# Layer 0's state-space mixer: the scan of a chunk's decays is pinned to its written place in VectorE's order

## The chip, the core and the metric

The kernel runs on one core of a Trainium2 chip. The metric is device microseconds (us) for one execution of the whole program, four layers deep; the time of a kernel is the median of its runs. Lower is better.

## The reference, cut to what matters

Four layers act on x, 4 sequences of 512 tokens with 256 channels. Each layer computes `x = x + attn(xn) + ffn(xn)` with `xn = layernorm(x)`. The change lies in layer 0, whose "attention" is a state-space mixer (Mamba2) with 32 heads of 64 channels and a state of 128. For each head and token t the reference does

```
h = dA[t] * h + (dt[t] * x[t]) (outer) B[t]
y[t] = h . C[t]
```

and then adds `D * x`, multiplies by silu(gate), normalises and projects back to 256 channels. Beside it, layer 0 has a gated feed-forward (256 to 1024 to 256) on the same xn. Layers 1 to 3 (latent attention with product-key experts; a head mixer with routed experts; full attention with top-p experts) are not touched.

## The kernel before, in words

**Tiling.** The recurrence over time is cut into chunks of 128 tokens. Work goes by group of 8 heads: 4 sequences x 4 groups = 16 groups `i`, each with 4 chunks `t`, so 64 chunks `c = 4i + t`. Inside a chunk the recurrence becomes matrix products: `G[s, h, t]`, the product of the decays from token s to token t, times `CB`, the product of B and C, is a 128x128 matrix for each head, and `y = G' x` (L486). What earlier chunks contribute comes through the state `S` (L468, L476, L481, L482).

**How G is made.** `decays` (L403) loads the chunk's decay rows from DRAM, broadcast to 128 partitions (tile `G`, 3 buffers, 512 KB a load, issued on SyncE's queue, SP, L406). `before` (L413) runs a scan on VectorE (DVE) over it with an identity as second operand (L421): it turns the row of single decays into running products, 128x1024 elements, in place. `before_gpsimd` (L443) multiplies by `CB` on GpSimd (POOL, L447). TensorE (PE) reads the result in L486, which frees the buffer.

**The loop.** `mamba_pieces` is software-pipelined by hand. The body for chunk c issues, in written order: for the next group, two projections (t = 0) or one (t = 1, 2) or none (t = 3) (`group`, L134, with ScalarE, ACT, at L276 and L400); the load of G for chunk c+2 (`decays`); the scan for chunk c+1 and its transposes (`before`, L421, L427, L429 and the loads of `eb`, L437); the convolution taps of the projections on DVE (L280, three for each projection); `within` for chunk c (L468, L469, L470 on POOL, G times CB for chunk c+1 on POOL L447, `xw` for chunk c+1 on POOL L450, L476, S, L486, then L491 and L492 on DVE, and the `ssq` sums on POOL, L496 to L499); and `project_out` for chunk c-1 (L507, added on DVE at L513). The feed-forward (L134 with tile `wu`, L201, L202, L212, added to x on DVE at L158) is woven in between by `weave`, which gives the next piece to the stream that is furthest behind by hand-written costs. After four groups of one sequence, the result is normalised (L152) and, when the feed-forward is also through, layernormed (L102, L103, L110).

**What sets the order on an engine.** Each engine runs its instructions strictly in a listed order and waits at the first one that isn't ready. The framework's scheduler makes these lists: it may move an instruction against its neighbours of the same engine as data dependencies and buffers allow. `tc.keep_in_program_order(...)` pins an instruction to its written place among the pinned ones. In the kernel before, the eight matmuls of L486 and the add L491 of each chunk are pinned; the scan L421 is not.

**PSUM.** The pools are "mm" with 4 buffers, "tr" with 2 and "acc" with 2. "tr" is shared by the transposes L427 (freed by L429), the projection L507 (freed by L513) and the feed-forward's output L212 (freed by L158).

Of the kernel before, what the change touches and what calls it, by code (L numbers as in the profile page):

```python
# [82 lines left out]
def v3(ap, b):  # L83
    return ap.rearrange("p (a b) -> p a b", b=b)
# [161 lines left out]
def mamba_pieces(c, a, ws, open_pool):  # L246
# [4 lines left out]
    nc, tc = c.nc, c.tc  # L251
# [161 lines left out]
    def before(i, t):  # L413

        b, g = i // 4, i % 4
        CT, Btok, CB, acc, ssq = seqs[b]
        w, wo, xc, sg = groups[i]
        tt, hs, cols = b * TPB + t, slice(g * HG, (g + 1) * HG), slice(t * P, (t + 1) * P)
        G = Gs.pop((i, t))
        flat = G.rearrange("p h t -> p (h t)")  # L420
        nc.vector.tensor_tensor_scan(  # L421
            flat, flat, eye.rearrange("p h t -> p (h t)"), 0.0, ALU.mult, ALU.add
        )

        pt = c.ps("tr")
        for k in range(4):
            nc.tensor.transpose(pt[:, k * P : (k + 1) * P], xc[:, k, cols], c.ident)  # L427
        xdt = c.tile(pool, [P, 512], "xdt")
        nc.vector.tensor_mul(v3(xdt, HD), v3(pt, HD), by_head(dt[:, tt, hs]))  # L429
        eb = None  # L430
        xD = c.tile(pool, [P, 4, P], "xD")
        for k in range(4):
            nc.scalar.mul(xD[:, k, :], xc[:, k, cols], d_par[:, 4 * g + k : 4 * g + k + 1])  # L433
        if t > 0:
            eb = c.tile(pool, [P, 4, P], "eb")
            for half in range(2):
                nc.sync.dma_start(  # L437
                    eb[half * HD : (half + 1) * HD],
                    since[tt, g * HG + half : (g + 1) * HG : 2, :].partition_broadcast(HD),
                )  # L440
        chunks[i, t] = [G, xdt, None, xD, eb]
# [93 lines left out]
    decays(0, 0)  # L535
    decays(0, 1)
    before(0, 0)
    before_gpsimd(0, 0)
    behind = None
    for i in range(16):  # L540
        for t in range(TPB):
            if t == 1 and i % 4 == 3 and i < 15:
                yield from sequence(i // 4 + 1)
            taps = []
            for k in ((0, 1), (2,), (3,), ())[t] if i < 15 else ():
                taps.append(group(i + 1, k))
                yield 3.4
            n = 4 * i + t + 1
            if n < 63:
                decays((n + 1) // 4, (n + 1) % 4)  # L550
            if n < 64:
                before(n // 4, n % 4)
            yield 0.5
            for tap in taps:
                tap()
            y = within(i, t)
            yield 2.6
            if behind:
                project_out(*behind)
                yield 1.7  # L560
            behind = i, t, y
# [1246 lines left out]
```

## Time and profile before

| what | us |
| --- | --- |
| median of 3 runs | 3154.67 (3148.51 to 3159.28) |
| the profiled execution's own time | 3156.7 |
| its span in the trace | 3154.9 |
| layer 0's scans, first to last start | 77.2 to 801.9 |
| PE busy in 100 to 800 | 683.5 of 700 |
| DVE busy in 100 to 800 | 549.4 of 700 |
| mean granted TensorE clock | 0.992 |

A row of the trace gives start, duration, engine, source line, output tile and inputs, and, where the engine stood idle before, for how long and on what. Matmul rows overlap, since they are pipelined: their starts count more than their durations. A PE row of 128x512 starts 0.43 us after the one before it when nothing holds PE up, though the row says 0.6 us. The four lines L427, L468, L476, L486 tell which chunk PE is at: t = 0 has no L468, t = 3 has no L476.

### The profile page before, as it was taken

The page shows a single profiled execution, that of the slowest core. Times are in us where ns is not written, and L with a number is a line of the kernel's source. Part 1 is how long each engine was busy: PE and PEld are TensorE (multiplying, and loading weights), DVE is VectorE, ACT ScalarE, POOL GpSimd, SP SyncE. Part 2 cuts the span into 40 slices and gives each one's busy share as a digit, 9 for nine tenths or more (in the row PEclk, how much of TensorE's full clock was granted, in tenths as well). Part 3 has the DMA queues.
Part 4 walks back from the last instruction along what each step waited for, and adds up shares of the span by engine and source line. Part 5 has one row for each costly group of instructions (what it writes and reads, how often), then busy time and mean ns, then how long its engine had stood idle before and what let it go on. Part 6 is the DMA issues. An engine that isn't in the chain of part 4 may idle for free.

```text
span 3154.9 us, 35717 instructions
## 1 busy us (share of the span) xinstructions
PE 3082.5 (98%) x12502; PEld 1885.9 (60%) x12502; DVE 1841.9 (58%) x4656; ACT 1249.8 (40%) x2898; POOL 627.9 (20%) x521
## 2 busy tenths in 40 slices
PE   8999999999899999999999999999999999999999
PEld 5566566565655555555676656566566655555555
DVE  5778778777677787787666555554555522222222
ACT  4444435444356666666525333333333311111111
POOL 0465455555400123331223000000000000000000
PEclk9999999999899999999999999999999999999999
DMA  4233333332310234444233000000000000000000
GB/s 131 77 100 124 93 94 111 103 104 77 118 37 13 80 99 117 101 112 138 80 100 103 4 21 7 1 27 1 21 1 1 20 21 20 20 20 20 0 0 27
DMA packets 89090, 185.15 MB, mean 59 GB/s; under 512 B 14192, under 2 KB 57216, under 8 KB 84176
## 3 DMA queue, kind: packets, MB, share of 16 engines
q1 hardware_dynamic: 74448, 135.05, 13.4%
q0 software_dynamic: 14176, 47.01, 6.2%
q8 instruction: 99, 1.62, 0.2%
q10 hardware_dynamic: 288, 0.82, 0.1%
q14 instruction: 79, 0.65, 0.1%
HBM read 160.95 MB, written 12.98 MB: 55 GB/s over the span
## 4 chain that ended last, share of the span: by engine, by line
PE 79%; DVE 11%; DMA 5%; ACT 2%; POOL 2%; issue 2%; SPq 1%; DVEq 0%; ACTq 0%; POOLq 0%
PE mm L134 30%; PE acc L212 9%; PE mm L643 7%; PE mm L142 5%; PE acc L1116 4%; PE acc L659 4%; DMA G<-own 3%; DVE G L421 2%; PE tr L1108 2%; DVE cy L280 2%; PE tr L824 2%; PE tr L507 2%; PE acc L868 2%; PE mm L1446 1%; PE tr L212 1%
## 5 line engine op out<-in xcount | busy, mean ns | idle before, releaser
L134 PE MATMUL mm<-xnT,wu 128*128 128x512 f32 x2128 | 953.3, 595 | 4.2 <-DVE cy L280 2.0
L134 PEld LDWEIGHTS mm<-xnT,wu 128*128 128x128 f32 x2128 | 399.3, 191 | 468.7 <-issue 435.8
L650 ACT ACTIVATE pr<-pr,nm 128x128 f32<-128x128 f32 (+3 forms) x512 | 285.7, 558 | 306.9 <-DVE nm L646 304.5
L202 DVE TENSOR_TENSOR hT<-sg,mm 128x512 f32<-128x512 f32 x176 | 120.6, 685 | 386.3 <-PE mm L134 372.1
L201 ACT ACTIVATE sg<-mm 128x512 f32<-128x512 f32 x176 | 104.6, 594 | 591.5 <-PE mm L134 591.3
L646 DVE CUSTOM_DVE_ANT_0 pr<-mm,late 128x128 f32<-128x128 f32 (+3 forms) x512 | 245.4, 483 | 82.6 <-PE mm L643 80.9
L212 PE MATMUL acc<-wu,hT 128*128 128x256 f32 x1280 | 286.6, 380 | 0.3 <-DVE hT L167 0.3
L212 PEld LDWEIGHTS acc<-wu,hT 128*128 128x128 f32 x1280 | 241.7, 190 | 49.1 <-issue 17.7
L134 PE MATMUL mm<-xnT,w_in 128*128 128x512 f32 x512 | 230.8, 597 | 0.0
L986 POOL DMA_INDIRECT e<-in_p_experts,ids x128 | 128.4, 1003 | 454.1 <-DVE x L152 413.4
L421 DVE TENSOR_TENSOR_SCAN G<-G,eye 128x1024 f32<-128x1024 f32 x64 | 156.0, 2437 | 64.9 <-DMA G<-own 64.8
L447 POOL TENSOR_TENSOR G<-G,CB 128x1024 f32<-128x1024 f32 x64 | 151.5, 2368 | 172.3 <-DVE G L421 95.9
L643 PE MATMUL mm<-kf,qf 128*128 128x128 f32 (+3 forms) x512 | 177.2, 445 | 6.1 <-DVE qf L801 3.7
L280 DVE SCALAR_TENSOR_TENSOR cy<-mm,ws,cy 128x511 f32<-128x511 f32 (+2 forms) x216 | 158.6, 741 | 34.9 <-ACT cy L276 31.4
L643 PE MATMUL mm<-k,q 128*128 128x128 f32 (+3 forms) x512 | 176.5, 434 | 1.0 <-DVE q L1081 1.0
L134 PEld LDWEIGHTS mm<-xnT,w_in 128*128 128x128 f32 x512 | 97.5, 192 | 103.3 <-issue 97.2
L433 ACT ACTIVATE xD<-xc,ws 128x128 f32<-128x128 f32 x256 | 84.2, 391 | 180.6 <-POOL y L470 164.2
L152 DVE SCALAR_TENSOR_TENSOR x<-acc,cw,x 128x256 f32<-128x256 f32 x128 | 62.0, 484 | 153.6 <-PE acc L212 153.5
L1116 PE MATMUL acc<-PT,V 128*128 128x512 f32 (+3 forms) x512 | 149.1, 433 | 0.0
L1081 DVE TENSOR_SCALAR q<-mm,bias 128x512 f32<-128x512 f32 x64 | 48.0, 751 | 165.1 <-PE mm L134 165.1
L824 PEld LDWEIGHTS tr<-con,pr 128*128 128x128 f32 x640 | 79.4, 142 | 95.0 <-ACT pr L817 30.2
L507 PE MATMUL tr<-wo,y 128*128 128x256 f32 x512 | 126.5, 390 | 6.9 <-DVE x L158 3.8
(310 smaller groups left out, 4926.8 us busy)
## 6 DMA issues: line engine op xcount, KB each, us to landing
G<-own SPq DMA_DIRECT2D x64, 512.0 KB, 4.4
w_in<-in_m_units SPq DMA_DIRECT2D x16, 1024.0 KB, 5.1
eb<-since SPq DMA_DIRECT2D x96, 128.0 KB, 3.4
wu<-in_o_units SPq DMA_DIRECT2D x8, 1536.0 KB, 6.5
wo<-in_m_units SPq DMA_DIRECT2D x16, 512.0 KB, 4.1
psw<-pes SPq DMA_DIRECT2D x128, 64.0 KB, 2.8
wu<-in_g_units SPq DMA_DIRECT2D x4, 1536.0 KB, 6.8
wu<-in_f_units SPq DMA_DIRECT2D x4, 1536.0 KB, 7.3
```

Of the source, the lines that this page charges most:

```text
L134: c.nc.tensor.matmul(out, lhsT=w[:, d, cols], rhs=c.xnT[:, d, tokens], start=(d == 0), stop=(d == 1))
L142: c.nc.tensor.matmul(out, lhsT=c.xnT[:, d, tokens], rhs=w[:, d, cols], start=(d == 0), stop=(d == 1))
L212: nc.tensor.matmul(po[:, j, :], lhsT=hT[k][:, (t + j) * P : (t + j + 1) * P], rhs=wd[:, k, :], start=(i == 0), stop=(i == per - 1),)
L280: nc.vector.scalar_tensor_tensor(y[:, j:], src[:, : SEQ - j], conv[:, k, 3 - j : 4 - j], y[:, j:], ALU.mult, ALU.add,)
L421: nc.vector.tensor_tensor_scan(flat, flat, eye.rearrange("p h t -> p (h t)"), 0.0, ALU.mult, ALU.add)
L447: nc.gpsimd.tensor_mul(G, G, seqs[b][2][:, t, :][:, None, :].to_broadcast([P, HG, P]))
L507: nc.tensor.matmul(po, lhsT=y[:, k, :], rhs=groups[i][1][:, k, :], start=(k == 0), stop=(k == 3))
L643: nc.tensor.matmul(sc, lhsT=q[:, i * P : n], rhs=k[:, :n], start=True, stop=True)
L646: nc.vector.tensor_tensor_reduce(out=pr, in0=sc, in1=late[:, SEQ - n :], scale=1.0, scalar=-NEG, op0=ALU.add, op1=ALU.min, accum_out=nm,)
L650: nc.scalar.activation(pr, pr, AF.Exp, bias=nm, scale=-1.0, accum_out=total)
L824: nc.tensor.transpose(pt[:, (i - j) * P : (i - j + 1) * P], prs[s][i][:, j * P : (j + 1) * P], c.ident)
L1116: nc.tensor.matmul(z[:, j * P :], lhsT=head["V"][:, j, h, :], rhs=head["PT"][:, j, j * P :], start=(j == 0), stop=(j == TPB - 1),)
```

## The change

One call is wrapped: the scan of `before` is pinned.

```diff
-        nc.vector.tensor_tensor_scan(
+        tc.keep_in_program_order(nc.vector.tensor_tensor_scan(
             flat, flat, eye.rearrange("p h t -> p (h t)"), 0.0, ALU.mult, ALU.add
-        )
+        ))
```

No instruction is added or taken away on DVE: both lists have the same 64 scans and the same shapes. What moves, by the two kernels' instruction lists:

- DVE before: nearly everywhere the slot after L492 of chunk c-1 holds the scan of chunk c+2, one chunk ahead of its written place, in front of the taps and of L429 of body c. In t = 3 bodies the slot is after L469 instead.
- DVE after: that slot holds the scan of chunk c+1. In t = 3 bodies it stands ahead of L429 and L469. At the start of layer 0, three scans stood among the taps of the first group; after, the taps come first, then one scan, L158, L429, then the second scan.
- Near the end of layer 0, two adds L158 (and L513 after them) stood behind a scan; after, they stand ahead of it. The last scan stands two chunks before the end in the list before, and one chunk later in the list after.
- Where a layernorm falls into layer 0, the scan that stood ahead of it in the list before stands behind it in one place in the list after.
- POOL follows: each G times CB (L447) is that of chunk c+1 and not of chunk c+2. In t = 3 bodies the list before has `xw` (L450), `y` (L470), then G; the list after has G, `xw`, `y`.
- SP keeps the order of the G loads; some halves of the `eb` loads (L437) move across a G load. PE, ACT: single neighbours swap, on PE mostly at the hand-over to layer 1.

## The prediction

> **What bounds the kernel now.** I read the page's busy shares first, then what PE waited for inside layer 0, then what DVE waited for there, then the timeline at the gaps.
>
> ```profile
> PE 3082.5 (98%) x12502; PEld 1885.9 (60%) x12502; DVE 1841.9 (58%) x4656; ACT 1249.8 (40%) x2898; POOL 627.9 (20%) x521
> ```
>
> PE is busy for 3082.5 of 3154.9 us, and in layer 0 its matmuls start back to back. So a change can give only what PE loses: its waits, and the slower clock after them. The view of PE's waits between 100 and 780 us:
>
> ```profile
> PE tr L507 <- DVE x L158: 3.8, 2, 2.3
> PE tr L507 <- DVE acc L513: 2.7, 3, 1.0
> PE tr L368 <- ACT BT L284: 2.6, 2, 1.9
> PE mm L134 <- DVE cy L280: 2.0, 3, 1.2
> PE tr L121 <- DVE xdt L429: 1.0, 1, 1.0
> PE mm L134 <- ACT sg L400: 0.6, 1, 0.6
> ```
>
> (Total us, times, longest.) They add up to 12.7 us. At the start (77 to 100 us) PE waits 2.4 us more, for ACT xc L284, and between 780 and 815 us 7.2 us, twice for L158. All of it in layer 0's loop: 22.3 us, 0.7% of the span. Nearly all lead to a late DVE, and DVE's waits in the same 100 to 780 us say what makes it late:
>
> ```profile
> DVE G L421 <- DMA G<-own: 62.3, 42, 2.9
> DVE y L491 <- POOL y L470: 36.8, 37, 3.6
> ```
>
> 42 scans stand at the head of DVE's list before their data has landed. The mechanism, at the largest gap of the middle, in the timeline (start, duration, engine, line, and idle before it):
>
> ```profile
> 694.44 2.29 DVE L421 TENSOR_TENSOR_SCAN G<-G,eye 128x1024 f32<-128x1024 f32 x1 [2.90 <-DMA G<-own]
> 696.65 0.67 DVE L158 TENSOR_TENSOR x<-tr,x 128x512 f32<-128x512 f32 x1
> 697.37 2.92 PE L507 MATMUL tr<-wo,y 128*128 128x256 f32 x8 [2.28 <-DVE x L158]
> ```
>
> The scan, of chunk c+2, waits 2.90 us for its load, issued only when L486 of chunk c-1 had freed the buffer. L158 is ready but queued behind it, it holds a "tr" buffer, and PE stands for 2.28 us.
>
> **The change, part by part.** DVE gains and loses no instruction; each slot gets the scan of one chunk less ahead. The load of that chunk was issued one body earlier (64 chunks lie in 95 to 815 us, 11.3 us each) and lands 4.4 us after its issue by the page's DMA table: about 7 us to spare. I cost the scans' waits as gone.
>
> *1. The first group (70 to 100 us).* Three scans (2.28 at 77.22, 2.28 at 83.34, 4.03 at 86.18) stand among the taps that PE's first transposes need. After, the last three taps are bound by their ACT L276, which ends at 87.24: taps to 89.5, xc L284 by 90.2, and the last transpose can follow PE's L212, which ends at 91.7, instead of starting at 94.57. PE's waits of 0.54 and 1.90 there go. The granted clock is 0.83 in 90 to 100, and the next 16 matmuls took 8.38 us where 16 elsewhere take 7.03: 1.35 more. Gain 0.54 + 1.90 + 1.35 = **3.8**. Late next: the first L486 needs scan (to 91.8) and POOL (2.36, to 94.2), while PE has 16 projections (6.9 us) in front of it: covered.
>
> *2. The middle (100 to 780 us).* Six PE gaps stand directly behind a scan that waited (gap | the scan's wait): at 362.6 1.49 | 1.83, at 435.3 0.66 | 1.48, at 595.7 0.82 | 0.90, at 621.1 1.92 | 2.90, at 697.4 2.28 | 2.90, at 742.8 0.82 | 1.26. The scan's wait is the longer one in each, so all six go: **8.0**. The one at 697.4 also lowers the clock (0.91 and 0.92 in 690 to 710): 2.92 us against 1.99 for the same 8 matmuls, then 7.63 against 7.03: **1.5**. The other 4.7 of the 12.7 come in bodies with six taps or beside a layernorm (232, 372 to 380, 419), where DVE has work and not a wait just before; earlier waits made it late, but not alone. I take half, **2.3**; ends 0 and 4.7.
>
> *3. The bodies with t = 3.* Here a new wait comes. POOL now has scan, then G, then xw, then y in front of L491; before, y was added first:
>
> ```profile
> 131.31 0.68 DVE L469 TENSOR_TENSOR y<-acc,eb 128x512 f32<-128x512 f32 x1
> ...
> 133.21 1.26 POOL L470 TENSOR_TENSOR y<-y,xD 128x512 f32<-128x512 f32 x1
> 133.50 3.13 DVE L421 TENSOR_TENSOR_SCAN G<-G,eye 128x1024 f32<-128x1024 f32 x1 [1.51 <-DMA G<-own]
> ...
> 136.55 0.66 DVE L491 TENSOR_TENSOR y<-acc,y 128x512 f32<-128x512 f32 x1
> 136.77 2.35 POOL L447 TENSOR_TENSOR G<-G,CB 128x1024 f32<-128x1024 f32 x1 [2.30 <-DVE G L421]
> 137.25 2.43 DVE L492 TENSOR_TENSOR y<-y,sg 128x512 f32<-128x512 f32 x1
> ```
>
> Before, from the end of the t = 2 body at 130.79 to the end of L492 at 139.68: 8.9 us, with a wait of 1.51, a scan stretched to 3.13 and L492 stretched from 0.69 to 2.43 beside POOL's G. After: 2.29 + 0.1 + 2.36 + 1.04 + 1.26 + 0.03 + 0.69 + 0.69 = 8.5, since POOL is idle at L492. Three other t = 3 bodies (from 173.4, 269.0 and 458.1) took 9.1 each. So DVE stands about 3.4 us waiting for POOL, but is not later than before: **0**, ends -2 and the rival below.
>
> *4. The last four chunks (780 to 820 us).* The two gaps behind L158 (3.51 and 3.70) shrink, because L158 now stands ahead of its scan. But DVE is the bound here (no projections for PE to do), it runs four scans where it ran three, and POOL's G and xw are next to be late. Followed by hand with the rows' durations from 783.3 us, where L492 ends: scan at 784.3, PE waits for xw till 790, L158 at 797.4, scans at 798.5 and 807.3, S by 804 and 812.7, and the last L469 at 815.6, where it was at 817.54. Gain **2**; ends -3 and 7.2 + 3.2 (the clock's 0.85 and 0.83 there: 1.12 + 1.49 + 1.35 against 0.60 + 0.68 + 1.09, and as much again) = 10.
>
> *5. SP, ACT and PE lists.* Neighbours swap; the eb loads have over a body of lead. Layer 1 simply starts earlier. 0, ends -2 and 2.
>
> Sum: 3.8 + 8.0 + 1.5 + 2.3 + 0 + 2 = 17.6. The profiled execution took 3156.7 (span 3154.9 and 1.8 around it), so 3139.1; it stands 2.0 above the median of the three runs, so on the median's scale **3137**.
>
> **Two rules of the Trainium skill.** "TensorE: Matmul & The Clock Gate", section on HAM oscillation, says that PE drops to half clock only when it idles for more than about 3.4 us. The clock row of 690 to 710 us shows a drop after 2.28 us, so here the trace decides; by the rule alone the clock terms of the gaps at 94 and 697 would be no gain of this change, and the sum 2.9 less. "SBUF — State Buffer", section on who interferes with whom, speaks against the change: a VectorE operation with two SBUF inputs and a GpSimd operation that reads SBUF exclude each other for a whole instruction. The 3.13 us scan beside POOL's y above fits it. After, the scan in t = 3 bodies starts while POOL has two ssq adds of 0.73 to run; by the rule each could hold the scan up by as much, which would turn the -0.4 of part 3 into about +0.3.
>
> **Rivals.**
>
> *PE never waits.* All 22.3 us go, with the clock's 1.35 + 1.5 + 3.2: 28.4, so 3126. For it: DVE is busy only 549 of 700 us and loses 62.3 waiting for loads. Against: the tail has one scan more, and the layernorm's burst is still DVE work.
>
> *The wait only changes its name.* DVE's gain in t = 0 to 2 is eaten by the wait for POOL in t = 3, and PE's gaps move rather than go; only the start gains: 3154.7 - 3.8 = 3151. For it: the rows from 303 to 313 us, where DVE, 1.36 us earlier, would wait for ACT L276 at 306.4 and gain nothing. Against: the six gaps each end with the scan's wait.
>
> *Slower.* In the t = 3 bodies L492 stays stretched (2.43 for 0.69) although POOL's G comes earlier, because ssq or xw meet it. Then DVE is 8.5 + 1.7 - 9.0 = 1.2 us later at 15 hand-overs to a t = 0 body. The point from which it decides: at 327 us the first taps end at 326.90 and PE takes their "mm" buffer at 327.29, 0.4 us to spare, so 0.8 us of it reaches PE: 12 us, and with the tail's end at -3 and the start's 3.8: 11 slower, 3166. Against: POOL is idle 1 to 3 us before each ssq in that place.
>
> That the pin does nothing is excluded: the instruction lists differ in nearly all 64 slots.
>
> **Chances.** Forecast 0.55 (own range 3129 to 3146), PE never waits 0.15, name changes 0.18, slower 0.12. From 3123 to 3157 all but the slower one and some edges are held. 0.3%, 9.5 us, is about what a measurement of this kernel can tell from no change: below 3145.2 lie 0.50 of the forecast and the first rival, 0.65; within, 0.05 + 0.18 and a little of the slower case, 0.25; above 3164.1, 0.10.
>
> **What would show it.** Right: DVE's wait for DMA at L421 falls from 64.8 us to under 10; the six gaps are missing; PE's waits in 100 to 780 fall from 12.7 to 2 to 4; the last L469 of layer 0 comes some 17 us earlier. POOL's y grows as DVE's releaser to 60 or more: part 3. Wrong: PE waiting for L280 in every t = 0 body (slower), or G times CB as the releaser of L486.

## The result, and the profile after

The change made the kernel slightly slower. Fifteen runs of the changed kernel have a median of 3164.6 us (3156.29 to 3171.02), fifteen of the kernel before beside them 3157.49 us (3148.51 to 3166.84): a ratio of 1.0022, 95% interval 1.0011 to 1.0032. The forecast was 3137 us with a range up to 3157, so both the time and the range missed. The profiled execution took 3165.98 us (span 3164.2), 9.3 more than that of before.

From the page, the busy shares, the group of POOL's products and that of the scans (busy us, mean ns of one, and the idle time before them):

```profile
PE 3085.8 (98%) x12502; PEld 1888.4 (60%) x12502; DVE 1837.0 (58%) x4656; ACT 1245.6 (39%) x2898; POOL 637.8 (20%) x521
...
L447 POOL TENSOR_TENSOR G<-G,CB 128x1024 f32<-128x1024 f32 x64 | 151.9, 2374 | 245.9 <-DVE G L421 245.9
...
L421 DVE TENSOR_TENSOR_SCAN G<-G,eye 128x1024 f32<-128x1024 f32 x64 | 155.7, 2432 | 0.0
```

The same two groups before:

```profile
L421 DVE TENSOR_TENSOR_SCAN G<-G,eye 128x1024 f32<-128x1024 f32 x64 | 156.0, 2437 | 64.9 <-DMA G<-own 64.8
L447 POOL TENSOR_TENSOR G<-G,CB 128x1024 f32<-128x1024 f32 x64 | 151.5, 2368 | 172.3 <-DVE G L421 95.9
```

The scan's line now ends in 0.0: VectorE's 64.8 us of waits for the loads are gone entirely. In the POOL line, 245.9 us of idle time are ended by the scan, where it was 95.9: POOL's product G times CB runs as soon as its scan has ended. VectorE's waits in layer 0 (95 to 830 us; total us, times, longest):

```profile
DVE y L491 <- POOL y L470: 81.8, 44, 4.7
DVE cy L280 <- ACT cy L276: 39.8, 30, 1.6
```

The wait for POOL's y has nearly doubled, from 42.2 us. And PE's waits between 60 and 860 us, the longest ones:

```profile
PE acc L468 <- DVE S L482: 6.7, 4, 2.9
PE mm L134 <- DMA tok<-xn_tokens: 4.0, 1, 4.0
PE tr L368 <- ACT BT L284: 4.0, 3, 1.6
PE mm L476 <- POOL xw L450: 3.4, 2, 3.1
PE tr L121 <- DVE xdt L429: 3.1, 1, 3.1
```

Of the two groups at L507 that led the list of before only 0.3 us is left. New names stand in their place: S (L482), xw (L450) and xdt (L429). Between 100 and 780 us PE's gaps add up to 16.2 us, where before had 12.7.

**Where the time went.** PE's order is nearly the same in both kernels, so the start of the eight L486 of a chunk can be laid side by side, chunk by chunk (0 to 63), and then layer 1's first projection, L134 of `pw`. The comparison is aligned at the first PE gap (L134 for ACT sg, at 71.85 us before and 71.94 after). A negative number is earlier than before:

| at | after minus before, us | what happened since the row above |
| --- | --- | --- |
| chunk 0 | -4.3 | the start's gain |
| chunk 3 | -2.7 | gap at L468 for S, 1.32 |
| chunk 23 | +0.6 | gaps of 1.19 and 1.25, others |
| chunk 24 | -4.2 | gaps of before at 362 to 380 us missing |
| chunk 33 | -1.2 | gaps of 1.35, 1.16 and 1.25 |
| chunk 34 | +3.8 | L121 for xdt, 3.14, and a slower clock behind it |
| chunk 58 | -0.2 | gaps of before at 595, 697 and 743 us missing or smaller, new ones elsewhere |
| layer 1's first L134 | +7.1 | the tail |

So the start gained what was forecast, the middle lost 4.1 net where 11.8 of gain were forecast, and the tail lost 7.3. Three of the middle's gaps are of one size and at one place of the loop: at the hand-over from body t = 2 to t = 3, in groups 0, 3 and 7 (at 127, 268 and 456 us). The rows of the changed kernel from 121 to 128 us (VectorE, POOL, then PE):

```profile
121.11 2.28 DVE L421 TENSOR_TENSOR_SCAN G<-G,eye 128x1024 f32<-128x1024 f32 x1
123.31 0.66 DVE L429 TENSOR_TENSOR xdt<-tr,dt 128x512 f32<-128x512 f32 x1
...
124.49 1.95 DVE L481 TENSOR_TENSOR S<-S,etot 128x512 f32<-128x512 f32 x1
126.55 0.69 DVE L482 TENSOR_TENSOR S<-mm,S 128x512 f32<-128x512 f32 x1
...
123.54 2.36 POOL L447 TENSOR_TENSOR G<-G,CB 128x1024 f32<-128x1024 f32 x1 [7.18 <-DVE G L421]
125.86 1.71 POOL L470 TENSOR_TENSOR y<-y,xD 128x512 f32<-128x512 f32 x1
...
127.30 1.16 PE L468 MATMUL acc<-CT,S 128*128 128x128 f32 x8 [1.32 <-DVE S L482]
```

The scan ends at 123.4, POOL's product runs from 123.54 to 125.9, S times etot takes 1.95 us instead of 0.68 beside it, POOL's y comes after the product, and PE waits 1.32 us for S. In the kernel before, a product began at 123.76 too, but it was that of a later chunk, beside the taps, and S times etot came at 127.53, when the product had ended:

```profile
123.53 2.29 DVE L280 SCALAR_TENSOR_TENSOR cy<-mm,ws,cy 128x511 f32<-128x511 f32 x3
123.76 2.36 POOL L447 TENSOR_TENSOR G<-G,CB 128x1024 f32<-128x1024 f32 x1 [3.54 <-DVE G L421]
127.53 0.68 DVE L481 TENSOR_TENSOR S<-S,etot 128x512 f32<-128x512 f32 x1
```

**The theory** for the experiments: the loads were late, as the prediction said, and their waits did cost PE; but POOL's product, now one chunk later, takes the gain back, by standing ahead of y and xw in POOL's queue and beside S on VectorE. **The rival**: the price is VectorE's own, a scan of 2.3 us directly in front of taps, xdt and S. Each run below is compared with runs of the kernel before beside it (in e1 to e8 every kernel, that before included, took some 60 us longer, nearly all of it between 1500 and 1800 us in layer 2; why is open; so only ratios are compared across runs); "the tail" is chunk 58 to layer 1's first L134, read from the traces with the same alignment.

### The profile page after: what moved, and what is told of

Read it like the earlier page. It is cut to its first block, busy times and chain, and to the rows that moved or that the text cites. A ratio compares the mean times of both kernels' runs of the same rounds, so it can differ in the third digit from the quotient of the medians.

```text
span 3164.2 us, 35693 instructions
## 1 busy us (share of the span) xinstructions
PE 3085.8 (98%) x12502; PEld 1888.4 (60%) x12502; DVE 1837.0 (58%) x4656; ACT 1245.6 (39%) x2898; POOL 637.8 (20%) x521
## 4 chain that ended last, share of the span: by engine, by line
PE 80%; DVE 10%; ACT 3%; POOL 3%; DMA 2%; issue 1%; SPq 1%; DVEq 0%; ACTq 0%; POOLq 0%
PE mm L134 31%; PE acc L212 9%; PE mm L643 7%; PE mm L142 5%; PE acc L1116 4%; PE acc L659 3%; PE tr L1108 2%; PE tr L507 2%; PE tr L824 2%; DVE G L421 2%; PE acc L868 2%; PE tr L212 2%; PE mm L1446 1%; PE acc L486 1%; PE acc L882 1%
## 5 line engine op out<-in xcount | busy, mean ns | idle before, releaser
L134 PE MATMUL mm<-xnT,wu 128*128 128x512 f32 x2128 | 953.8, 596 | 4.1 <-ACT sg L400 2.8
L134 PEld LDWEIGHTS mm<-xnT,wu 128*128 128x128 f32 x2128 | 399.8, 191 | 469.2 <-issue 433.2
L134 PE MATMUL mm<-xnT,w_in 128*128 128x512 f32 x512 | 228.6, 593 | 0.0
L447 POOL TENSOR_TENSOR G<-G,CB 128x1024 f32<-128x1024 f32 x64 | 151.9, 2374 | 245.9 <-DVE G L421 245.9
L280 DVE SCALAR_TENSOR_TENSOR cy<-mm,ws,cy 128x509 f32<-128x509 f32 (+2 forms) x216 | 159.6, 742 | 54.6 <-ACT cy L276 50.8
L134 PEld LDWEIGHTS mm<-xnT,w_in 128*128 128x128 f32 x512 | 96.4, 190 | 101.8 <-issue 96.1
L824 PE MATMUL tr<-con,pr 128*128 128x128 f32 x640 | 122.2, 282 | 11.9 <-DVE PT L828 5.0
```

The costliest lines, as they stand in the source:

```text
L134: c.nc.tensor.matmul(out, lhsT=w[:, d, cols], rhs=c.xnT[:, d, tokens], start=(d == 0), stop=(d == 1))
L280: nc.vector.scalar_tensor_tensor(y[:, j:], src[:, : SEQ - j], conv[:, k, 3 - j : 4 - j], y[:, j:], ALU.mult, ALU.add,)
L447: nc.gpsimd.tensor_mul(G, G, seqs[b][2][:, t, :][:, None, :].to_broadcast([P, HG, P]))
L824: nc.tensor.transpose(pt[:, (i - j) * P : (i - j + 1) * P], prs[s][i][:, j * P : (j + 1) * P], c.ident)
```

## The experiments

### The change in one place at a time

The pin is kept in part: for all but the last four chunks' scans (e1), for those four alone (e2), for the first three alone (e3). The edit, for e1; e2 has `>= 60`, e3 `< 3`:

```diff
-        tc.keep_in_program_order(nc.vector.tensor_tensor_scan(
+        scan = nc.vector.tensor_tensor_scan(
             flat, flat, eye.rearrange("p h t -> p (h t)"), 0.0, ALU.mult, ALU.add
-        ))
+        )
+        if 4 * i + t < 60:
+            tc.keep_in_program_order(scan)
```

> The scan is pinned for the first 60 chunks and left to the scheduler for the last four. Theory: in the changed kernel's trace the last four chunks lost 8.4 us against the kernel before (PE's row of layer 1's first projection L134 went from 1.2 us early at the chunk of 789 us to 7.2 us late), because the last scans come one chunk later and scan, G on POOL, xw and y follow one another there. Then this kernel is 8 us faster than the changed one: about 1 us below the kernel before, -3 to +2. Rival: what is lost comes from L491 waiting for POOL in all bodies (81.8 us of DVE waits after, 36.8 before); then the tail holds only its share, 4 of 64 bodies, and this kernel stays 5 to 7 us above the kernel before.

Measured: 3224.88 us beside 3220.27, ratio 1.0014 (1.0004 to 1.0024). Chunk 58 stands at +0.1 (the changed kernel: -0.2), and the tail still lost 5.5 us: the freed scheduler put the last scans into a third order, with gaps of 5.63 and 4.63 us at 796 and 817 us. Neither expectation's reason came true, so this run says only that freeing the tail does not restore it.

> The scan is pinned for the last four chunks only. Theory (the tail costs it): 6 to 9 us slower than the kernel before. Rival (the loss is spread over all bodies): 0 to 1 us slower.

Measured: 3221.03 us beside 3220.27, ratio 1.0003 (0.9993 to 1.0012). In the trace chunk 58 stands at -0.2 and the tail costs 3.6 us, with the changed kernel's gaps (3.06 at L476's place for POOL's xw, 2.16 for S, 2.20 for y). So the tail is a cost of its own by the trace. The time lies in the rival's range (0 to 1 us slower) and does not show it.

> The scan is pinned for chunks 0 to 2 only. Theory: the first L486 comes 4.2 us earlier, as in the changed kernel, and the kernel is 3 to 4 us faster than the kernel before. Rival: what the start gains is eaten before the end of layer 0, since DVE's waits for the loads set the pace of the middle: within 1 us of the kernel before.

Measured: 3217.67 us beside 3220.27, ratio 0.9996 (0.9984 to 1.0007). Chunk 0 comes 4.3 us sooner; then 3.3 are lost at chunks 2 and 3 in gaps of 1.54 and 1.33, where one order passes into the other. The start's gain is there in the trace, and mostly given back two chunks later; the time does not resolve what is left of it.

### The scan later still (e4)

The scan of chunk c+2 is pinned directly ahead of the add L491 of chunk c, so that its load has always landed and POOL's product follows into y times sg:

```diff
+    def scan(i, t):
+        flat = Gs[i, t].rearrange("p h t -> p (h t)")
+        tc.keep_in_program_order(nc.vector.tensor_tensor_scan(...))
...
+        if 4 * i + t + 2 < 64:
+            scan((4 * i + t + 2) // 4, (t + 2) % 4)
         tc.keep_in_program_order(nc.vector.tensor_add(y, v3(ya, P), y if t > 0 else xD))
```

> The scan is pinned in another place: the scan of chunk c+2 (as far ahead as in the kernel before) directly ahead of the add L491 of chunk c (line numbers here shift by 4), where its load has had most of a body to land and where DVE waits for POOL's y. Theory: DVE's waits for loads hurt only because they stand at the head of a body; here both they and the late G of the changed kernel are gone. The six gaps go and the tail keeps its two scans of lead: 8 to 15 us faster than the kernel before, DVE's wait for G's load under 10 us. Rival: PE's gaps come from DVE's work in bursts, not from its waits, and only move: within 4 us of the kernel before.

Measured: 3261.69 us beside 3220.27, ratio 1.0131 (1.0116 to 1.0145). VectorE waits for no load, and only 30.8 us for POOL's y, and yet the kernel is 41 us slower, far outside both expectations. The rows of its trace (L443 is the product here, L496 is y times sg):

```profile
173.34 2.56 DVE L452 TENSOR_TENSOR_SCAN G<-G,eye 128x1024 f32<-128x1024 f32 x1
175.82 0.66 DVE L495 TENSOR_TENSOR y<-acc,y 128x512 f32<-128x512 f32 x1
...
176.74 2.21 DVE L496 TENSOR_TENSOR y<-y,sg 128x512 f32<-128x512 f32 x1
...
176.05 2.35 POOL L443 TENSOR_TENSOR G<-G,CB 128x1024 f32<-128x1024 f32 x1 [2.29 <-DVE G L452]
```

L496 starts 0.7 us into the product and ends 0.5 us after it. All 64 of them took 2016 ns on average, where before has 905. That is 71 us of VectorE in 64 chunks. How much of the 41 us is this stretch is not separated: the scan itself also stands ahead of the add here, and PE waits 9.4 us for that add. So what a scan's end releases on POOL may cost more than the wait that the place avoids; the next pair tests the product alone.

### POOL's product made short (e6, e7)

The product is done for one head of eight, in the kernel before and in the changed one; the other seven heads keep the bare decays. Every engine's order stays what it was in each:

```diff
-        nc.gpsimd.tensor_mul(G, G, seqs[b][2][:, t, :][:, None, :].to_broadcast([P, HG, P]))
+        nc.gpsimd.tensor_mul(G[:, :1], G[:, :1], seqs[b][2][:, t, :][:, None, :].to_broadcast([P, 1, P]))
```

> The kernel before, with POOL's product G*CB done for one head of eight (7 heads keep the bare decays, so this part of the computation is left out); every engine's order is as in before. It is the partner of the next run and gives the base for it. Both theories: a few us faster than before, ratio 0.996 to 1.000, since VectorE's instructions beside the 2.4 us product are no longer stretched; VectorE still waits some 60 us for G's loads.

> The changed kernel, with the same product done for one head of eight (the other 7 are left out as in its partner); every engine's order is as in the changed kernel. Theory (the change's price is POOL's product, which comes a chunk later, stands ahead of xw and y and stretches S): the gaps L468<-S and the tail's L476<-POOL xw go, and this is faster than its partner by 8 us or more (start 4, six gaps of 8 us in part), ratio to partner 0.9975 or less. Rival (the price is the scan itself in its new place on VectorE, 2.3 us in front of taps, xdt and S): within 3 us of the partner.

Measured: before's order 3210.9 us, ratio 0.9975 (0.9963 to 0.9987); the changed order 3200.24 us, ratio 0.9938 (0.9924 to 0.9952), both beside 3217.87. The changed order is 10.7 us the faster of the two (0.9963 by the ratios, about 0.0018 either way), where with the full product it is 7.1 the slower. So the theory held, and this is the experiment that carries the case. In the changed order's trace, the same place as above:

```profile
123.17 0.45 POOL L447 TENSOR_TENSOR G<-G,CB 128x128 f32<-128x128 f32 x1 [7.73 <-DVE G L421]
...
124.13 0.68 DVE L481 TENSOR_TENSOR S<-S,etot 128x512 f32<-128x512 f32 x1
...
125.66 1.16 PE L468 MATMUL acc<-CT,S 128*128 128x128 f32 x8
```

VectorE's scan is where it was, 2.28 us in front of xdt and S; only the product is short, S is 0.68 again and PE's L468 has no wait. PE's gaps in 100 to 780 us: 12.5 us in before's order with the short product, 5.5 in the changed order. That is near the 2 to 4 that the prediction had named for the changed kernel, and layer 1 begins 6.3 us sooner than in the partner (the rest of the 10.7 is within what the times can tell). So the late loads did cost PE, and the scan's new place by itself is a gain: as the price of the change, the rival falls. At two places it holds, since two gaps outlive the short product (PE's waits, 60 to 860 us, in the changed order):

```profile
PE acc L468 <- DVE S L482: 2.9, 1, 2.9
PE tr L121 <- DVE xdt L429: 1.9, 1, 1.9
```

The first is the last chunk's, 2.87 us as in the changed kernel; the second is what is left of 3.14 at the layer norm (see e10). There the scan on VectorE, ahead of xdt and S, is enough to make PE wait.

### The order on POOL (e8)

The change's place for the scan is kept; POOL's y, product and xw are held to the program's order, y first:

```diff
-            nc.gpsimd.tensor_add(y, y, xD)
+            tc.keep_in_program_order(nc.gpsimd.tensor_add(y, y, xD))
...
-        nc.gpsimd.tensor_mul(G, G, seqs[b][2][:, t, :][:, None, :].to_broadcast([P, HG, P]))
+        tc.keep_in_program_order(nc.gpsimd.tensor_mul(G, G, ...))
```

(and xw in the same way.)

> The changed kernel, with POOL held to the program's order: the sum y of a chunk goes ahead of the product G*CB of the next. Theory (the product ahead of y is what VectorE waits for): its waits at L491 for POOL's y fall from 82 us to 45 or less, and the middle comes back by 2 to 6 us, the tail's L476<-POOL xw stays or grows: ratio to before 0.9995 to 1.0015. Rival (VectorE's waits for y cost PE nothing, being slack): the waits fall, the time stays within 1.5 us of the changed kernel's, ratio 1.0015 to 1.003.

Measured: 3227.25 us beside 3217.87, ratio 1.0025 (1.0015 to 1.0035). VectorE's waits for y fall from 82 to 33.3 us and nothing is won. One reason is on VectorE: y times sg now meets the product. Its group in this run, then in the changed kernel (95 to 830 us):

```profile
L492 DVE TENSOR_TENSOR y<-y,sg 128x512 f32<-128x512 f32 x64 | 111.2, 1737 | 1.7
L492 DVE TENSOR_TENSOR y<-y,sg 128x512 f32<-128x512 f32 x64 | 55.2, 863 | 1.8
```

That is 56 us more of VectorE, for 49 us of waits saved. PE's waits for S fall to 0.7, and this stands in their place:

```profile
PE acc L486 <- POOL G L447: 6.8, 7, 1.5
PE mm L476 <- POOL xw L450: 5.6, 4, 2.9
```

With y first, the product is late for PE; with the product first, y and S are. The time lies in the rival's range. But that the wait for y was slack for PE this run does not show, since a stretch took the wait's place; e5 below speaks for it.

### Two halves of the product (e13), and the changed kernel again (e14)

What is left open by these runs: does the product harm by holding single VectorE instructions beside it, or because POOL's queue as a whole is late? The product is cut into two instructions of four heads:

```diff
-        nc.gpsimd.tensor_mul(G, G, seqs[b][2][:, t, :][:, None, :].to_broadcast([P, HG, P]))
+        for h in (slice(0, 4), slice(4, 8)):
+            nc.gpsimd.tensor_mul(G[:, h], G[:, h], seqs[b][2][:, t, :][:, None, :].to_broadcast([P, 4, P]))
```

> The changed kernel, with POOL's product G*CB as two instructions of four heads each. If a VectorE instruction is held for as long as one POOL instruction lasts, the longest S and y*sg fall from 2.0 to 2.4 us to about 1.3, the four gaps L468<-S of 1.25 us in bodies with t=3 fall under 0.3 each, and layer 0 ends 3 to 6 us sooner than in the changed kernel (ratio to it 0.998 to 0.999). If POOL's queue as a whole is late, the halves follow each other without a break, VectorE is held again by the second half, and nothing changes (ratio to the changed kernel 0.9995 to 1.0005; POOL's two halves take 0.1 us more).

> The changed kernel once more, on the chip of these runs: both theories 1.001 to 1.003 of the kernel before; it is the base for the run with two halves.

Measured beside 3156.77 us: with halves 3165.68, ratio 1.0025 (1.0013 to 1.0037); the changed kernel 3163.28, ratio 1.0021 (1.0009 to 1.0033), its gaps in layer 0 nearly all as in the first trace. The halves' trace at the same hand-over (lines are one further on; L482 is S times etot, L487 the eight matmuls):

```profile
124.39 0.87 DVE L482 TENSOR_TENSOR S<-S,etot 128x512 f32<-128x512 f32 x1
125.37 0.69 DVE L483 TENSOR_TENSOR S<-mm,S 128x512 f32<-128x512 f32 x1
127.65 0.69 DVE L492 TENSOR_TENSOR y<-acc,y 128x512 f32<-128x512 f32 x1 [1.59 <-POOL y L471]
...
123.44 2.95 POOL L448 TENSOR_TENSOR G<-G,CB 128x512 f32<-128x512 f32 x2 [7.48 <-DVE G L421]
126.36 1.26 POOL L471 TENSOR_TENSOR y<-y,xD 128x512 f32<-128x512 f32 x1
...
126.11 1.16 PE L469 MATMUL acc<-CT,S 128*128 128x128 f32 x8 [0.23 <-DVE S L483]
128.40 1.09 PE L487 MATMUL acc<-G,xdt 128*64 128x128 f32 x16 [1.12 <-DVE y L492]
```

The first mechanism is there: S times etot takes 0.87 instead of 1.95, PE's wait for S is 0.23 instead of 1.32, and y times sg is 720 ns on average (863 in the changed kernel). But 2.3 us later PE waits 1.12 for y, behind POOL's y, behind the product. L487 begins at 128.40, where L486 of the changed kernel began at 128.38. The other two hand-overs went the same way (0.17 and 1.13 us, 0.16 and 1.12). So at these places the time is set by the sum of POOL's work between the scan and PE, and the stretched S is only where it showed. Both expectations named a piece of this; on the time the second was right.

### The tail's product (e11)

The changed kernel, the short product in the last four chunks only:

```diff
+        hs = 1 if 4 * i + t >= 60 else HG
-        nc.gpsimd.tensor_mul(G, G, seqs[b][2][:, t, :][:, None, :].to_broadcast([P, HG, P]))
+        nc.gpsimd.tensor_mul(G[:, :hs], G[:, :hs], seqs[b][2][:, t, :][:, None, :].to_broadcast([P, hs, P]))
```

> The changed kernel, with POOL's product G*CB done for one head of eight in the last four chunks alone (the other 7 heads of these chunks keep the bare decays, so this part of the computation is left out). Theory (in the tail POOL's chain scan, product, xw is PE's limit): from chunk 58 to layer 1's start 6 us or more less than in the changed kernel, ratio to before 0.9995 to 1.0008. Rival (the tail waits for VectorE's scans): less than 3 us, ratio 1.001 to 1.003.

Measured: 3156.2 us beside 3161.74, ratio 0.9986 (0.9973 to 1.0). From chunk 58 to layer 1's first L134 the trace gains 2.8 us on before, where the changed kernel lost 7.3: a difference of 10.1 us, more than the 6 that the theory asked for, and the ratio too is below its range. Some of it may be recovery: this execution had lost 3.2 us more than the changed kernel before chunk 58, most of it at a longer gap of 2.27 us at L368, where the products are still whole. Layer 1 begins 6.9 us sooner than in the changed kernel. In the changed kernel the tail's rows are these:

```profile
801.47 3.20 DVE L421 TENSOR_TENSOR_SCAN G<-G,eye 128x1024 f32<-128x1024 f32 x1
...
799.67 2.85 POOL L447 TENSOR_TENSOR G<-G,CB 128x1024 f32<-128x1024 f32 x1
802.48 3.02 POOL L450 TENSOR_TENSOR xw<-xdt,after 128x512 f32<-128x512 f32 x1
...
805.56 1.12 PE L476 MATMUL mm<-xw,Btok 128*128 128x512 f32 x2 [3.06 <-POOL xw L450]
812.64 1.09 PE L486 MATMUL acc<-G,xdt 128*64 128x128 f32 x16 [0.82 <-DVE y L491]
818.57 2.08 PE L468 MATMUL acc<-CT,S 128*128 128x128 f32 x8 [2.87 <-DVE S L482]
```

Scan, product and xw follow one another on two engines, and scan and xw, side by side, are both stretched (xw 3.02 against 1.04 alone, the scan 3.20 against 2.28). PE has no projections left to fill the time, and nothing behind these gaps absorbs them. With the short product the wait for xw is gone; of the last one, for S, 2.02 us stay, so that one is mostly VectorE's own scan, xdt and S.

### One scan at the layer norm (e10)

The largest single loss of the middle: two scans stand close together at 491.59 and 496.78 us, behind the layer norm's burst, the second directly in front of a tap and xdt, and PE's L121 waits for xdt:

```profile
494.96 1.89 DVE L492 TENSOR_TENSOR y<-y,sg 128x512 f32<-128x512 f32 x1
496.78 2.28 DVE L421 TENSOR_TENSOR_SCAN G<-G,eye 128x1024 f32<-128x1024 f32 x1
499.62 0.67 DVE L429 TENSOR_TENSOR xdt<-tr,dt 128x512 f32<-128x512 f32 x1
...
500.35 1.05 PE L121 MATMUL tr<-con,xn 128*128 128x128 f32 x4 [3.14 <-DVE xdt L429]
501.20 1.06 PE L468 MATMUL acc<-CT,S 128*128 128x128 f32 x4
502.05 1.91 PE L476 MATMUL mm<-xw,Btok 128*128 128x512 f32 x2
```

Only the scan of chunk 35 is put behind its xdt:

```diff
+        if (i, t) != (8, 3):
+            scan()
...
         nc.vector.tensor_mul(v3(xdt, HD), v3(pt, HD), by_head(dt[:, tt, hs]))
+        if (i, t) == (8, 3):
+            scan()
```

> The changed kernel, with the scan of one chunk alone, 35, behind its xdt in place of ahead of it. Theory (in the changed kernel too the scan held ahead of xdt in that burst cost the 3.1 us gap and the clock behind it, 5.0 us in all): chunk 35 comes 3 to 5 us sooner (the scan now stands ahead of S there, up to 1.3 us back), ratio to before 1.0005 to 1.0015. Rival (given back a few chunks later): 1.0015 to 1.003.

Measured: 3163.93 us beside 3161.74, ratio 1.0001 (0.9993 to 1.001). The gap falls from 3.14 to 1.51, the next L486 comes 3.3 us sooner, 1.1 go back at S behind the moved scan, and layer 1 begins 2.9 us sooner than in the changed kernel. The direction is the theory's, and the ratio is a little better than it asked for. The time's difference to the changed kernel (6.6 by the ratios, about 4.4 either way) is more than the trace shows, and only 2.9 of it has a place.

### The load a body sooner (e5, e9, e15) and its control (e12, e16)

Before's slots for the scans in the steady bodies, but each load issued a body sooner into a fourth buffer. S and sq have one buffer, to make room:

```diff
-        G = c.tile(pool, [P, HG, P], "G", bufs=3)
+        G = c.tile(pool, [P, HG, P], "G", bufs=4)
...
+            c_ = 4 * i + t
+            if c_ < 61:
+                decays((c_ + 3) // 4, (c_ + 3) % 4)
+            if 0 < c_ < 62:
+                scan((c_ + 2) // 4, (c_ + 2) % 4)
```

> The kernel before's order of VectorE in the steady bodies (the scan of a chunk's decays two chunks ahead, at the head of a body), but G has a fourth buffer, so each broadcast load is issued a whole body sooner; to make room S and sq have one buffer in place of two. Only in body 0 do the first scans stand behind the taps, as in the changed kernel. Theory (late loads did cost PE the six gaps of before, 8.0 us, and the clock at 697 us, 1.5 us, and the changed kernel lost them again by putting POOL's product a chunk later): VectorE's waits for DMA under 10 us of 64.8, PE's six gaps mostly gone, no new gaps of S or of POOL's xw in the tail, layer 1 starts 10 to 15 us sooner, ratio to before 0.995 to 0.997. Rival (the gaps come from VectorE's work itself, and a load that comes sooner only lets the next thing be waited for): only the start's 4 us, ratio 0.998 to 1.000.

Measured: 3210.95 us beside 3217.87, ratio 0.9971 (0.9961 to 0.9981). VectorE waits for no load; the gaps of before at 362, 411, 595, 697 and 743 us are missing or halved; but the 3.13 us gap at the layer norm is here too, since these scans are pinned in the same way, and layer 1 begins 7.5 us sooner where the theory said 10 to 15. VectorE's wait for POOL's y is 77.8 us, as high as in the changed kernel, in a kernel that is faster than the one before, and here y times sg is not stretched (752 ns on average): so most of that wait is slack for PE.

e9 moves two scans at the layer norm's burst as well (chunks 36 and 37, behind body 34's work and behind body 35's xdt).

> The kernel with G's fourth buffer, with two scans moved at the one place where a layer norm of the other stream fills VectorE: the scan of chunk 36 stands behind the work of body 34 (not at its head, in front of taps and xdt), that of chunk 37 behind xdt of body 35. Theory (the scan held ahead of xdt in that burst is what made PE wait 3.1 us at L121 and lose clock behind it): that gap goes, chunk 35 comes 4 to 5 us sooner, layer 1 starts some 12 us sooner than in before, ratio 0.995 to 0.9965. Rival (the burst itself is too much for VectorE, whatever the order): another gap of 2 us or more within the next three chunks, ratio as without it, 0.9965 to 0.998.

Measured: 3152.54 us beside 3161.74, ratio 0.9966 (0.9955 to 0.9977). The 3.13 us gap falls to 1.52, and two of 1.0 follow within three chunks; layer 1 begins 9.5 us sooner than in before. The ratio lies where the two expectations meet; in the rows each was half right.

The control has before's scans and the buffer counts alone:

```diff
-                S = state[i] = c.tile(pool, [P, 512], "S")
+                S = state[i] = c.tile(pool, [P, 512], "S", bufs=1)
...
-        sq = c.tile(pool, [P, 4, P], "sq")
+        sq = c.tile(pool, [P, 4, P], "sq", bufs=1)
```

> The kernel before, with one buffer for S and for sq in place of two and nothing else, as the control of the runs with G's fourth buffer. Both theories: no effect, layer 0's gaps as in before, ratio 0.999 to 1.001. If it came out at 0.998 or less, the gain of the fourth buffer would be from here.

Measured: 3152.77 us beside 3161.74, ratio 0.9972 (0.996 to 0.9983). This was not expected. It takes the proof from e5: the time of e5 is no better than that of its control. The traces do differ. Up to layer 1's first L134 the control gains 3.5 us (1.5 at the start, most of the rest because the wait of 3.14 us for `tok` is missing there), e5 7.5; between chunk 0 and chunk 58 the control loses 1.9 and e5 gains 1.3. So the early load is worth some 3 to 4 us of layer 0 by the trace, and this is not shown by the time. The control's further gain comes behind layer 0: at 885 us it stands at -10.1 with the alignment, so 6.6 us come in the first 55 us of layer 1, whose start the scheduler ordered anew.

> The kernel with G's fourth buffer and the two scans moved at the layer norm's burst, with the product in two halves. If VectorE is held by single POOL instructions: 1 to 4 us faster than without the halves, ratio to before 0.9955 to 0.9965. If POOL's queue is what counts: as without, 0.996 to 0.9975; the tail's L478<-POOL xw gaps of 1.5 and 3.1 us stay under both.

> The kernel before with one buffer for S and sq, with the product in two halves. If VectorE is held by single POOL instructions, but mostly in the changed order: within 2 us of the same kernel without halves, ratio to before 0.9965 to 0.998. If POOL's queue is what counts: the same range or 1 us slower, so this run only says whether the price belongs to the changed order.

Measured beside 3156.77: e9 with halves 3152.08 us, ratio 0.9981 (0.9969 to 0.9992), layer 1 begins 8.2 sooner; the control with halves 3144.54 us, ratio 0.996 (0.9946 to 0.9975), layer 1 begins 4.4 sooner. The halves do not help the early load (e15 lies outside both of its ranges, on the slow side), and they cost the kernel with before's order nothing (e16 is 0.0005 better than its range). e5, e9, e12, e15 and e16 are faster than both kernels of the case, by 0.2 to 0.4% of the kernel before; which of them is best is not resolved, and for e12 and e16 most of the gain is not of the scans.

## Why the prediction was wrong, step by step

- **What bounds the kernel now: right, and incomplete.** The waits for the loads did hold VectorE, and PE behind it. That is shown by the pair with the short product, where PE's gaps fall from 12.5 to 5.5 us with the same change. What the view of VectorE's waits could not say is that POOL's chain from scan to PE was itself close to its limit.
- **Part 1, the start: right.** 3.8 forecast, 4.3 measured at chunk 0. 1.6 of it went at chunk 3, in the first wait for S.
- **Part 2, the middle: mostly right about what goes, wrong about what comes. This is the step that failed.** Four of the six gaps are gone or nearly so (362, 595, 697 and 743 us); the two at L368 stayed, 1.16 for 0.66 at 435 us and 1.60 for 1.92 at 621 us. Both end with BT from ScalarE, 3 us after the scan that had waited, so "directly behind a scan" was a wrong reading there. With the clock and the half of the others, 11.8 were forecast; between chunk 0 and 58, 4.1 were lost. The sum listed the gaps of the old order and put those of the new one at nothing. They measured 3.8 us for S at the three hand-overs, and 5.0 at the layer norm with the clock behind it (chunk 33 to 34), beside smaller ones.
- **Part 3, the t = 3 bodies: right in its own bodies, and blind one body earlier.** It put the new order (scan, product, xw, y) at 0, because L491 and L492 would end no later. That held: from the end of one L492 to the next, the 16 bodies with t = 3 took 9.66 us on average before and 9.46 after, and L492 is 0.68 to 0.69 us in all of them. But it watched y and sg there alone. S, which the t = 2 body computes for the next chunk's L468, was not followed. With the product directly behind the scan, S times etot met it at the end of the t = 2 body of groups 0, 3 and 7 (1.95 us for 0.68), and PE waited 1.2 to 1.3 us each time. And the sum was taken on VectorE's list alone: product and y are 4.1 us on POOL at that hand-over (2.36 and 1.71), while PE there has only L507, L427, L468 and L486 to do. e8 and e13 show that neither y first nor a product in halves saves this time.
- **Part 4, the tail: wrong sign.** -2 forecast with an end of +3, +7.3 measured. It named G and xw as "next to be late" and four scans instead of three, and then followed the rows by hand with their unstretched durations: xw took 3.02 us, a scan 3.20, the product 2.85. e11 prices the product there at 7 to 10 us.
- **Part 5:** 0 forecast; behind layer 0 the profiled execution lost 2 us more, its repetition (e14) won 0.9 back, so nothing of it can be put down to the change.
- **The layer norm's burst** was named only as a reason against the first rival. It cost the 5.0 us above; the short product (e7) took 1.2 off its gap, and moving the scan behind xdt (e10) 1.6, so product and scan share this price.
- **The rivals.** "PE never waits" did not come: 16.2 us of waits in the middle. "The wait only changes its name" was the nearest in kind: VectorE's 64.8 us for loads became 40 more for POOL, and PE's gaps moved. "Slower" had the right side and, by luck, nearly the right time (3166 for 3164.6), but the wrong place: it was added up from 12 us of PE waiting for L280, which came to 0.6; L492 was not stretched in the t = 3 bodies, S was a body earlier.
- **The signs named beforehand** came out as 0 us of DMA waits (under 10), 81.8 us for POOL's y (60 or more), but 16.2 us of PE waits (2 to 4), and the last L469 not 17 us earlier but 5 later. The first two are about VectorE and were right; they did not bear on the time.

On the clock: the gap of 3.14 us at 500 us was followed by two matmuls of 1.91 us that take 1.02 elsewhere, at a granted clock of 0.83 in 500 to 510 us. The Trainium skill, "TensorE: Matmul & The Clock Gate", section on HAM oscillation, names idle gaps above about 3.4 us as what drops the clock; here it dropped after 3.14, as it had after 2.28 in before.

On the ports: the Trainium skill, "SBUF — State Buffer", section on who interferes with whom, says that a VectorE operation with two SBUF inputs and a GpSimd operation that reads SBUF shut each other out for a whole instruction, and that the order of issue decides who waits. The rows agree: S at 1.95 and y times sg at 2.21 us beside a product of 2.36, 0.87 beside halves. The prediction weighed this rule at the scan, where it costs little, and not at S.

## What to carry to other kernels

Taking a wait away from an engine off the critical path is a gain only if no other limit stands right behind it: before moving an instruction, follow what its end releases on the other engines until the chain reaches the critical one, and add up that chain in the shortest body, with every instruction it will stand beside. Waits that grow by tens of us can be slack (POOL's y, 77.8 us in e5, which is faster than before with 42.2), and a wait that shrinks can come back as a stretched instruction (e8); the test is to make the suspected work short in both orders and compare the two, which here turned 7 us slower into 11 us faster. And a control for an edit's side conditions is worth a run: one buffer less, meant to be nothing, was worth as much as the edit it stood for.

## What the runs showed of the hardware beside this

- The same first matmuls on PE (14 and 16 of L142 at some 15 and 18 us) took 1.7 to 2.1 and 1.87 us in some executions, and 3.03 and 3.46 in others (e1, e10, e11, e12, e15, e16), though the view gives a granted clock of 1.00 to both; all that follows is then 5 to 6 us later. It can be a part of the 15 to 18 us between the extreme runs of one kernel. The Trainium skill, "TensorE: Matmul & The Clock Gate", section "What's actually happening", says that the clock's window runs free, so that the number of slow first matmuls differs from run to run; the durations fit this, the clock column does not show it.
- A product in two halves is not free: 1354 ns on average for each 128x512, 2.71 us for both, against 2374 ns in one (e13 and the changed kernel).
